# Group norm's last pieces and the weight turns one engine per step, and part of the last rounding to fp8 on GpSimd

## The chip, the cores and the metric

The kernel runs on one core of a Trainium2 chip. Its five engines each take their instructions from a queue of their own, in the order in which the program issued them: PE (TensorE, the matrix multiplier, whose results go to PSUM), DVE (VectorE), ACT (ScalarE), POOL (GpSimd) and SP (SyncE, used here to start DMAs). An engine that waits for another's result holds up everything behind it in its own queue. The metric is the device time of one execution in microseconds.

## The reference

The input is an image batch x of 4 x 64 x 64 positions with 96 channels; each image is a sequence of 4096 positions. Cut to what matters:

```python
# layer 0
xn   = layer_norm(group_norm(x, 32 groups of 3 channels))      # statistics of a whole image
proj = xn @ W_in + b_in                                        # 96 -> 3*96 + 3*96*16
h_t  = d_t * (A_t * h_{t-1}) + d_t * (B_t * u_t)               # a scan over 4096 positions, 96 x 16 states
y_t  = sigmoid(gate_t) * sum_over_16(C_t * h_t)
x    = x + y @ W_out + b_out
# layer 1
t = x + attention(layer_norm(x))                               # no softmax: q (k^T v), 6 heads
h = relu(q16(q8(ln(t)) @ q8(W1)^T) + q8(b1))                   # rounded to fp8 (5,2) before, fp16 after each product
t = t + q16(q16(q8(h) @ q8(W2)^T) + q8(b2))                    # 96 -> 384 -> 96
```

The group norm of an image needs sums over the whole image before its first position can be worked on, and the attention, being linear, needs a 97 x 97 matrix summed over the whole image before its first position can be finished.

## The kernel before

**Tiles and steps.** An image is cut into NCH = 8 chunks of 512 positions, so there are N = 32 chunks. A chunk's scan is cut into NT = 12 tiles of 128 partitions (32 channels times 4 states) by 512 positions. The main loop makes one *step* per tile, K = 384 in all. A step issues the tile's three projections (`project`, L269: three fp32r matmuls each, into the PSUM banks tagged A, B and C or D), ACT's copy of the B projection out of its single bank (`b_copy`, L811), POOL's product (`b_mul`, L814), DVE's product with d and bias (`a_mul`, L823), DVE's scan (L830), and the product with C on DVE (`c_mul`, L854) or on ACT and POOL (L860, L863).

**What hangs on the steps.** Everything else is put into a table `steps` by `at(step, fn)` and is issued at the end of that step. Offsets from a chunk's first step stand in the dictionary `AT`. `Front` prepares a chunk (group norm applied as `centre` and `scale` on POOL, L670 and L673; layer norm: `stats` L371 and L373 on DVE, `rstd` on POOL, L378 to L384, of which L392 is a power, `apply` on ACT, L396; `transpose`, L684; `affine`, `upper`, `low`; further projections). `tail` finishes a chunk of layer 0 (`state_sum` L878, `gated`, `project_out`, `residual` L926, a layer norm, `keep` L935 and `spill` of the transposed chunk to DRAM, `gram`). `attn_matrix` makes the image's 97 x 97 matrix `rmat`, and `ffn` does layer 1 of a chunk an image later: `fetch`, `attention` (L1076), `residual` (L1081), layer norm, `quant_in` (L1098), three products `hidden`, relu, rounding to fp8, `project_out` (L1133), `round_out`, `bias_out` (L1148), `total` (L1155), `store`. All PSUM tiles besides the projections share three banks tagged M; a new tile takes a bank that has been given back, and its first matmul waits for the last reader of the tile before.

**Group norm.** While image b is worked on, `group_norm(b+1, ...)` collects the sums of the next image: `first` (a chunk's mean as a shift, L564 and L566 on ACT), eight times `sums` (PE turns a chunk into a bank M) and `sums_out` (ACT, L574), and then a chain of small pieces. `moments` reduces on DVE (L581, L582) and goes on with three operations on POOL (L583 to L585); `mean` has a matmul (L590), two DVE operations (L592, L594) and, for images 1 to 3, two on POOL (L596, L597); `root` has a matmul (L602), one DVE operation (L604) and a power on POOL (L605); `diagonal` is on ACT (L612), `spread` on PE (L618), `spread_out` on ACT (L627). With e the step of the last `sums`, these stand at steps e+1, e+2, e+4, e+6, e+8 and e+8. All operations of a piece are issued in the same step, on three engines one after the other. For image 1, e is 57; for images 2 and 3 it is 149 and 245.

**Weight turns.** At steps 20, 32, 44 and 56 a matrix of layer 1 is turned by PE into a bank M and copied out by DVE in the same step; the last one, `weights_bias`, has four DVE operations (L355 to L359).

**The end.** Work whose step would be 384 or more is not put into the table. The last chunk's tail, what is left of image 2's layer 1 (chunks 5 to 7 above all) and all of image 3's layer 1 are given as jobs to a planner (`Plan`), each with an engine, an assumed cost and what it waits for. The planner lays out the jobs for a number of randomly disturbed priorities (`end.tries`), keeps the order that its own costs call the shortest, and issues the work in that order. For these chunks the relu is one DVE operation on fp16 (`relu_vector`, L1123), and `quant` (L1127) is one ACT operation that rounds a whole chunk, 128 x 1536, to fp8. In image 3 the layer norm of the even chunks is applied by DVE (L403) and of the odd ones by ACT (L396); `round_out` of the odd chunks is on DVE (L1141), of the even ones on ACT (L1143).

Of the kernel before, what the change touches and what calls it, by code (L numbers as in the profile page):

```python
# [63 lines left out]
def conv_attn_hybrid_kernel(  # L64
# [269 lines left out]
    def weights_attention():  # L334
        ps = bank("M", [C, CA], "wq_ps")
        nc.tensor.transpose(ps, w_qkv[:, 0:C], ident[:CA, :CA])
        nc.vector.tensor_copy(w_qt[0:C, :], ps)

    def weights_ffn1():
        ps = bank("M", [C, HID], "w1_ps")  # L340
        for m in range(NK):
            nc.tensor.transpose(ps[:, m * P : (m + 1) * P], w1_sb[:, m, :], ident)
        nc.vector.tensor_copy(w1_q, ps, saturate=False)

    def weights_ffn2():
        ps = bank("M", [P, NK, C], "w2_ps")
        for m in range(NK):
            nc.tensor.transpose(ps[:, m, :], w2_sb[:, m * P : (m + 1) * P], ident[:C, :C])
        nc.vector.tensor_copy(w2_q, ps, saturate=False)

    def weights_bias():
        ps = bank("M", [P, NK], "b1_ps")
        nc.tensor.transpose(ps, b1_sb, ident[:NK, :NK])
        b1_8 = small.tile([P, NK], F8, tag="b1_8", name="b1_8", bufs=1)
        nc.vector.tensor_copy(b1_8, ps, saturate=False)  # L355
        nc.vector.tensor_copy(b1_q, b1_8)
        b2_8 = small.tile([P, C], F8, tag="b2_8", name="b2_8", bufs=1)
        nc.vector.tensor_copy(b2_8, b2_sb, saturate=False)
        nc.vector.tensor_copy(b2_q, b2_8)  # L359
# [173 lines left out]
    class GroupNorm:  # L533
# [45 lines left out]
        def moments(self):  # L579
            t = small.tile([C, 2], F32, tag="gt", name=f"gt_{self.b}", bufs=2)  # L580
            nc.vector.tensor_reduce(t, self.s, AX.X, ALU.add)  # L581
            nc.vector.tensor_scalar_mul(t, t, 1.0 / L)  # L582
            nc.gpsimd.tensor_tensor(self.mv[:, 0:1], t[:, 0:1], self.c, ALU.subtract)  # L583
            nc.gpsimd.tensor_tensor(t[:, 0:1], t[:, 0:1], t[:, 0:1], ALU.mult)
            nc.gpsimd.tensor_tensor(self.mv[:, 1:2], t[:, 1:2], t[:, 0:1], ALU.subtract)  # L585


        def mean(self):
            ps = bank("M", [C, 2], f"gm_ps_{self.b}")
            nc.tensor.matmul(ps[:, 0:1], lhsT=third, rhs=self.mv[:, 0:1], start=True, stop=True)  # L590
            self.m = small.tile([C, 2], F32, tag="gm", name=f"gm_{self.b}", bufs=2)
            nc.vector.tensor_copy(self.m[:, 0:1], ps[:, 0:1])  # L592
            w = small.tile([C, 1], F32, tag="gw", name=f"gw_{self.b}", bufs=2)
            nc.vector.tensor_tensor(w, self.mv[:, 0:1], ps[:, 0:1], ALU.subtract)  # L594
            engine = nc.gpsimd if self.b else nc.vector
            engine.tensor_tensor(w, w, w, ALU.mult)  # L596
            engine.tensor_tensor(w, w, self.mv[:, 1:2], ALU.add)  # L597
            self.w = w

        def root(self):  # L600
            ps = bank("M", [C, 2], f"gv_ps_{self.b}")
            nc.tensor.matmul(ps[:, 0:1], lhsT=third, rhs=self.w, start=True, stop=True)  # L602
            v = small.tile([C, 1], F32, tag="gv", name=f"gv_{self.b}", bufs=2)
            nc.vector.tensor_scalar(v, ps[:, 0:1], 1e-5, None, ALU.add)  # L604
            nc.gpsimd.tensor_tensor(self.m[:, 1:2], v, mhalf[0:C, 0:1], ALU.pow)  # L605

# [22 lines left out]
    def group_norm(b, s0):  # L629
# [17 lines left out]
        for n in range(NCH):  # L647
# [3 lines left out]
            at(when[n] + AT["sums_out"] - AT["sums"], call, "sums_out", n)  # L651
        for n, name in ((1, "moments"), (2, "mean"), (4, "root"), (6, "diagonal"), (8, "spread"),
                        (8, "spread_out")):
            at(when[-1] + n, call, name)

# [237 lines left out]
    end.last = {}  # L893
    end.tries = 800

# [163 lines left out]
    def ffn(b, i, s0):  # L1059
# [6 lines left out]

        vector = b == B - 1 and i % 2 == 0

# [56 lines left out]
        def quant():  # L1125
            v["hq"] = sb("bu", [P, NK, TC], F8, f"hq_{nm}")
            nc.scalar.activation(v["hq"], v["h16"], AF.Copy, saturate=False)  # L1127

# [9 lines left out]
        def round_out():  # L1138
            v["y16"] = tile_of("y16", "xs", [P, J, C], F16, "y16")
            if phase["end"] and i % 2:  # L1140
                nc.vector.tensor_copy(v["y16"], v["ps"])  # L1141
            else:
                nc.scalar.copy(v["y16"], v["ps"])  # L1143

# [27 lines left out]
        if fetch not in done and b < B - 1:  # L1172
            at(K - 4, fetch)
            done.add(fetch)
# [24 lines left out]
        if hidden not in done:  # L1199
            r, h, c = [], None, None  # L1200
            for m in range(NK):
# [3 lines left out]
                        take=[f"rep:{nm}"] if m == 0 else [], free=[f"M:{m}{nm}"])  # L1205
                r.append(job("DVE", 0.5, relu_vector, m, after=[c]))
            a = job("ACT", 1.5, quant, after=r, take=[f"bu:q{nm}"], free=[f"rep:{nm}"])
        a = job("PE", 0.5, project_out, after=[a], take=[f"A:y{nm}"], free=[f"bu:q{nm}"])
        a = job(*(("ACT", 0.48) if vector else ("DVE", 0.56)), round_out, after=[a],
                take=[f"xs:{nm}"], free=[f"A:y{nm}"])  # L1210
# [11 lines left out]
    def planned_start():  # L1222
# [22 lines left out]
        a = job("DVE", 0.4, q.aggregate, after=a)  # L1245
        m = job("DVE", 1.1, q.mean, after=[a])
        r = job("DVE", 0.7, q.root, after=[m], late=0.9)
        g = []
# [119 lines left out]
    second = planned_start()  # L1368

    for n, fn in enumerate((weights_attention, weights_ffn1, weights_ffn2, weights_bias)):  # L1370
        at(NT + 8 + NT * n, fn)
    for b in range(B):
# [98 lines left out]
```

## Time and profile before

| | us |
|---|---|
| median of 3 runs | 1183.2 (1182.86 to 1183.66) |
| the profiled execution's own time | 1184.49 |
| its span in the trace | 1182.8 |
| PE busy | 1140.1 (96%) |
| DVE busy | 1113.2 (94%) |
| POOL busy | 1030.3 (87%) |
| ACT busy | 817.3 (69%) |

The span is the time from the first to the last instruction of the program; all stretches below are given in microseconds from its start. The steps run to about 1110; what follows is the planned end. "Busy" is time in which an engine executes; an instruction that waits is not busy. A row of the list of waits names the engine and line that waited, who released it, the total, the number of times and the longest. A row of a timeline has the start, the duration, the engine, the line, the operation, the tiles (out<-in), their shape, and in brackets how long the engine stood idle before it and what ended that. A row of the instruction groups ends in the busy time, the mean duration of one in ns, and the idle time before. A row of the table by stretch has the length, the busy time and count of instructions for PE, PEld (weight loads), DVE, ACT and POOL, then PE's granted clock, the DMA share and GB/s.

### The profile page before, as it was taken

How to read it: one execution, taken by the hardware profiler on the slowest of the kernel's cores; microseconds unless marked ns; L12 is line 12 of the kernel's file. 1: busy time of each engine (PE TensorE's matmuls, PEld its weight loads, DVE VectorE, ACT ScalarE, POOL GpSimd, SP SyncE). 2: the span in 40 equal slices, each digit the busy share in tenths (PEclk: the TensorE clock that was granted, in tenths of full speed). 3: DMA queues.
4: the chain of work that ended last, by engine and by line, in shares of the span. 5: the costliest groups of instructions: out<-in, count | busy, mean ns of one | idle time of the engine just before them, and what ended most of it. 6: DMA issues, size and time to landing. Idle time of an engine off the chain costs nothing. (4 is left out here: it accounts for less than half of the span.)

```text
span 1182.8 us, 19203 instructions
## 1 busy us (share of the span) xinstructions
PE 1140.1 (96%) x5899; PEld 874.6 (74%) x5899; DVE 1113.2 (94%) x2093; ACT 817.3 (69%) x1826; POOL 1030.3 (87%) x1176
## 2 busy tenths in 40 slices
PE   5999999999999999999999999999999999999885
PEld 4777777677777777777777777777777777777573
DVE  6999999899999999999999999999999999999865
ACT  4666655556556777877877777777776777776476
POOL 5798887788889899999999999999999999988554
PEclk8999999899999999999999999999999999999989
DMA  7676776687776776787777777766777778667221
GB/s 185 142 167 143 167 155 154 141 176 161 170 160 151 161 162 157 158 190 170 161 159 161 172 162 166 171 158 152 159 165 169 160 162 185 147 145 153 60 75 47
DMA packets 104288, 182.12 MB, mean 154 GB/s; under 512 B 42637, under 2 KB 50769, under 8 KB 104186
## 3 DMA queue, kind: packets, MB, share of 16 engines
q1 hardware_dynamic: 90060, 106.96, 37.3%
q0 software_dynamic: 13536, 73.93, 31.4%
q8 instruction: 46, 0.75, 0.3%
q14 instruction: 56, 0.46, 0.1%
q10 hardware_dynamic: 590, 0.02, 0.0%
HBM read 69.12 MB, written 24.77 MB: 79 GB/s over the span
## 5 line engine op out<-in xcount | busy, mean ns | idle before, releaser
L814 POOL TENSOR_TENSOR bu<-bu,rep 128x512 f32<-128x512 f32 x384 | 512.9, 1345 | 43.3 <-ACT state L840 34.8
L830 DVE TENSOR_TENSOR_SCAN h<-Aps,state,bu 128x512 f32<-128x512 f32 x336 | 426.2, 1268 | 0.7 <-POOL ch L863 0.5
L811 ACT ACTIVATE bu<-Bps,b_bac 128x512 f32<-128x512 f32 x384 | 263.1, 685 | 198.5 <-PE Bps L269 192.9
L823 DVE SCALAR_TENSOR_TENSOR Aps<-Aps,b_bac,rep 128x512 f32<-128x512 f32 x384 | 281.9, 734 | 8.2 <-PE Aps L269 8.2
L269 PE MATMUL Bps<-xs,w 128*128 128x512 f32 x768 | 268.0, 430 | 7.7 <-ACT bu L811 7.1
L269 PE MATMUL Aps<-xs,w 128*128 128x512 f32 x768 | 242.2, 396 | 1.2 <-DVE h L830 1.0
L863 POOL TENSOR_TENSOR ch<-ch,h 128x512 f32<-128x512 f32 x126 | 170.4, 1352 | 7.9 <-ACT ch L860 3.7
L269 PEld LDWEIGHTS Aps<-xs,w 128*128 128x128 f32 x768 | 143.9, 188 | 37.3 <-DVE h L830 3.0
L269 PEld LDWEIGHTS Bps<-xs,w 128*128 128x128 f32 x768 | 126.7, 191 | 51.2 <-ACT bu L811 15.4
L269 PE MATMUL Aps<-xl,w 128*128 128x512 f32 x384 | 152.0, 396 | 0.0
L269 PE MATMUL Bps<-xl,w 128*128 128x512 f32 x384 | 151.7, 395 | 0.0
L269 PE MATMUL Dps<-xs,w 128*128 128x512 f32 x384 | 121.0, 396 | 0.0
L269 PE MATMUL Cps<-xs,w 128*128 128x512 f32 x384 | 120.6, 395 | 0.0
L854 DVE SCALAR_TENSOR_TENSOR ch<-Dps,b_bac,h 128x512 f32<-128x512 f32 x160 | 118.6, 742 | 0.9 <-PE Dps L269 0.5
L869 POOL DMA_DIRECT2D ch<-ch x94 | 89.6, 953 | 0.3 <-DMA ch<-ch 0.3
L269 PEld LDWEIGHTS Bps<-xl,w 128*128 128x128 f32 x384 | 72.5, 189 | 17.7
L269 PEld LDWEIGHTS Dps<-xs,w 128*128 128x128 f32 x384 | 72.3, 188 | 17.7
L269 PEld LDWEIGHTS Aps<-xl,w 128*128 128x128 f32 x384 | 72.2, 188 | 17.7
L269 PEld LDWEIGHTS Cps<-xs,w 128*128 128x128 f32 x384 | 72.0, 188 | 17.6
L860 ACT ACTIVATE ch<-Cps,b_bac 128x512 f32<-128x512 f32 x94 | 64.6, 688 | 24.1 <-PE Cps L269 24.1
L269 PE MATMUL Dps<-xl,w 128*128 128x512 f32 x192 | 75.9, 395 | 0.0
L269 PE MATMUL Cps<-xl,w 128*128 128x512 f32 x192 | 75.8, 395 | 0.0
(200 smaller groups left out, 2045.2 us busy)
## 6 DMA issues: line engine op xcount, KB each, us to landing
ch<-ch POOLq DMA_DIRECT2D x94, 768.0 KB, 6.7
rep<-ddd SPq DMA_DIRECT2D x124, 384.0 KB, 7.4
ddd<-dd SPq DMA_DIRECT2D x31, 384.0 KB, 3.2
xl<-lo SPq DMA_DIRECT2D x62, 128.0 KB, 2.5
x<-in_x_dram SPq DMA_DIRECT2D x32, 192.0 KB, 3.0
xatd<-xat SPq DMA_DIRECT2D x32, 192.0 KB, 3.6
xal<-xatd SPq DMA_DIRECT2D x32, 192.0 KB, 2.8
out_dram<-o SPq DMA_DIRECT2D x32, 192.0 KB, 2.1
```

The lines of the kernel that those rows point to most:

```text
L269: nc.tensor.matmul(ps, lhsT=wt[:, n], rhs=mv, start=(n == 0), stop=(n == 2))
L811: nc.scalar.activation(self.bu, self.b_ps, AF.Identity, bias=self.bias(0))
L814: nc.gpsimd.tensor_tensor(self.bu, self.bu, rep[self.b, self.i][:, 1, self.cg], ALU.mult)
L823: nc.vector.scalar_tensor_tensor(self.a_ps, self.a_ps, self.bias(1), rep[self.b, self.i][:, 0, self.cg], ALU.add, ALU.mult,)
L830: nc.vector.tensor_tensor_scan(self.h, self.a_ps, self.bu, 0.0 if self.i == 0 else state[self.sh, self.cg], ALU.mult, ALU.add,)
L854: nc.vector.scalar_tensor_tensor(self.slot(), self.c_ps, self.bias(2), self.h, ALU.add, ALU.mult)
L860: nc.scalar.activation(self.ch, self.c_ps, AF.Identity, bias=self.bias(2))
L863: nc.gpsimd.tensor_tensor(self.ch, self.ch, self.h, ALU.mult)
L869: nc.gpsimd.dma_start(chs[g, 0], chs.pop((g, sh)), accum_op=ALU.add)
```

## The change

Three things are changed.

1. The group norm's chain is cut where the engine changes, into eleven pieces: moments (DVE), variances (POOL), group_sums (PE), mean (DVE), squares (POOL), group_sums (PE), offset (DVE), root (POOL), diagonal (ACT), spread (PE), spread_out (ACT). They stand one a step, at e+2, e+3, ... e+12. The PSUM tiles of group_sums and spread are now held from one step into the next. In the start of the kernel, which has a plan of its own, the pieces are called together in the old order.
2. Each weight turn's copy out of PSUM is issued one step after PE's transposes.
3. In the end, `quant` of the chunks with i % 3 != 0 is a POOL copy; DVE applies the layer norm only for i % 4 == 0 in image 3; all `round_out` are on ACT; the planner's cost of the relu is 0.47 for 0.5 and its tries are 1500 for 800. The fetch of image 2's last chunk is issued at step 383 for 380.

```diff
     def weights_attention():
         ps = bank("M", [C, CA], "wq_ps")
         nc.tensor.transpose(ps, w_qkv[:, 0:C], ident[:CA, :CA])
-        nc.vector.tensor_copy(w_qt[0:C, :], ps)
+        return lambda: nc.vector.tensor_copy(w_qt[0:C, :], ps)
...
             nc.vector.tensor_scalar_mul(t, t, 1.0 / L)
+            self.t = t
+
+        def variances(self):
+            t = self.t
             nc.gpsimd.tensor_tensor(self.mv[:, 0:1], t[:, 0:1], self.c, ALU.subtract)
...
+        def group_sums(self, name):
+            self.ps = bank("M", [C, 2], f"g{name}_ps_{self.b}")
+            nc.tensor.matmul(
+                self.ps[:, 0:1], lhsT=third, rhs=self.mv[:, 0:1] if name == "m" else self.w,
+                start=True, stop=True,
+            )
+
         def mean(self):
-            ps = bank("M", [C, 2], f"gm_ps_{self.b}")
-            nc.tensor.matmul(ps[:, 0:1], lhsT=third, rhs=self.mv[:, 0:1], start=True, stop=True)
+            ps = self.ps
...
+        def squares(self):
+            w, engine = self.w, nc.gpsimd if self.b else nc.vector
             engine.tensor_tensor(w, w, w, ALU.mult)
             engine.tensor_tensor(w, w, self.mv[:, 1:2], ALU.add)
-            self.w = w
+
+        def offset(self):
+            self.v = small.tile([C, 1], F32, tag="gv", name=f"gv_{self.b}", bufs=2)
+            nc.vector.tensor_scalar(self.v, self.ps[:, 0:1], 1e-5, None, ALU.add)

         def root(self):
-            ps = bank("M", [C, 2], f"gv_ps_{self.b}")
-            nc.tensor.matmul(ps[:, 0:1], lhsT=third, rhs=self.w, start=True, stop=True)
-            v = small.tile([C, 1], F32, tag="gv", name=f"gv_{self.b}", bufs=2)
-            nc.vector.tensor_scalar(v, ps[:, 0:1], 1e-5, None, ALU.add)
-            nc.gpsimd.tensor_tensor(self.m[:, 1:2], v, mhalf[0:C, 0:1], ALU.pow)
+            nc.gpsimd.tensor_tensor(self.m[:, 1:2], self.v, mhalf[0:C, 0:1], ALU.pow)
...
-        for n, name in ((1, "moments"), (2, "mean"), (4, "root"), (6, "diagonal"), (8, "spread"),
-                        (8, "spread_out")):
-            at(when[-1] + n, call, name)
+        chain = (
+            ("moments",), ("variances",), ("group_sums", "m"), ("mean",), ("squares",),
+            ("group_sums", "v"), ("offset",), ("root",), ("diagonal",), ("spread",), ("spread_out",),
+        )
+        for n, args in enumerate(chain):
+            at(when[-1] + AT["sums_out"] - AT["sums"] + 1 + n, call, *args)
...
-    end.tries = 800
+    end.tries = 1500
...
-        vector = b == B - 1 and i % 2 == 0
+        vector = b == B - 1 and i % 4 == 0
...
             v["hq"] = sb("bu", [P, NK, TC], F8, f"hq_{nm}")
-            nc.scalar.activation(v["hq"], v["h16"], AF.Copy, saturate=False)
+            if i % 3 == 0:
+                nc.scalar.activation(v["hq"], v["h16"], AF.Copy, saturate=False)
+            else:
+                nc.gpsimd.tensor_copy(v["hq"], v["h16"], saturate=False)
...
-            if phase["end"] and i % 2:
-                nc.vector.tensor_copy(v["y16"], v["ps"])
-            else:
-                nc.scalar.copy(v["y16"], v["ps"])
+            nc.scalar.copy(v["y16"], v["ps"])
...
-            at(K - 4, fetch)
+            at(K - 1, fetch)
...
-                r.append(job("DVE", 0.5, relu_vector, m, after=[c]))
-            a = job("ACT", 1.5, quant, after=r, take=[f"bu:q{nm}"], free=[f"rep:{nm}"])
+                r.append(job("DVE", 0.47, relu_vector, m, after=[c]))
+            a = job(*(("ACT", 1.5) if i % 3 == 0 else ("POOL", 1.6)), quant, after=r, take=[f"bu:q{nm}"], free=[f"rep:{nm}"])
...
+    def turned(step, fn):
+        at(step + 1, fn())
+
     for n, fn in enumerate((weights_attention, weights_ffn1, weights_ffn2, weights_bias)):
-        at(NT + 8 + NT * n, fn)
+        at(NT + 8 + NT * n, turned, NT + 8 + NT * n, fn)
```

`weights_ffn1`, `weights_ffn2` and `weights_bias` are changed as `weights_attention` is; the four DVE operations of `weights_bias` become a function `biases_out` that its lambda calls.

## The prediction

> **What bounds the kernel now.** I read the page first: PE is busy 96% of the span, DVE 94%. Between 230 and 1100 PE never rests, so there only a stall of PE, or work for PE, can move the time. The rest I looked for where the change works: the group norm chains (193 to 230 for image 1, 455 to 475 and 729 to 750 for images 2 and 3) and the end (1110 to 1177).
>
> The waits between 193 and 230 name what PE lost beside image 1's chain:
>
> ```profile
> PEld Bps L269 <- ACT bu L811: 3.0, 1, 3.0
> PE Bps L269 <- ACT bu L811: 2.6, 1, 2.6
> POOL gmv L583 <- DVE gt L582: 2.0, 1, 2.0
> ACT z L396 <- POOL nmr_c L384: 1.5, 1, 1.5
> PE xnt_ps L684 <- POOL bu L814: 0.9, 1, 0.9
> ```
>
> The timeline of that stall, in order of time:
>
> ```profile
> 207.45 0.58 POOL L605 TENSOR_TENSOR gm<-gv,mhalf 96x1 f32<-96x1 f32 x1
> ...
> 212.07 1.54 ACT L396 ACTIVATE z<-z,nmr_c,rstd_c 128x96 f32<-128x96 f32 x4 [1.53 <-POOL nmr_c L384]
> ...
> 213.51 0.63 ACT L612 ACTIVATE gdg<-ident,gm 96x96 f32<-96x96 f32 x2
> ...
> 214.88 0.67 ACT L811 ACTIVATE bu<-Bps,b_bac 128x512 f32<-128x512 f32 x1
> ...
> 215.61 1.22 PE L269 MATMUL Bps<-xs,w 128*128 128x512 f32 x2 [2.56 <-ACT bu L811]
> ```
>
> ACT's b_copy (L811), which frees the only bank B, stands behind a layer norm that waits for POOL, the chain's diagonal (L612) and the next image's `first`. The table by stretch shows what followed:
>
> ```profile
> 172.00:178.80 6.80, 5.71 (x26) 4.14 (x24) 6.80 (x16) 5.00 (x13) 5.78 (x9) 1.00 0.83 184
> 208.17:214.99 6.82, 4.87 (x24) 3.44 (x22) 6.29 (x14) 3.99 (x13) 6.65 (x10) 1.00 0.66 133
> 214.99:221.82 6.83, 6.21 (x17) 5.10 (x18) 3.86 (x4) 1.73 (x5) 3.58 (x3) 0.50 0.84 213
> ...
> 1142.00:1173.70 31.70, 23.17 (x190) 15.73 (x186) 21.39 (x75) 30.30 (x52) 17.09 (x24) 1.00 0.18 50
> ```
>
> After 6.8 us with 1.95 of them idle PE ran at clock 0.50 for 6.83 us; a stretch with 1.09 idle was followed by clock 1.00. The last row is the end: from 1142 ACT works 30.3 of 31.7 us, POOL 17.1. The groups of 1114 to 1178:
>
> ```profile
> L1127 ACT ACTIVATE hq<-h 128x1536 fp8e5<-128x1536 f16 x11 | 16.1, 1494 | 0.1
> L396 ACT ACTIVATE xn<-x,nmr_f,rstd_f 128x96 fp8e5<-128x96 f32 x24 | 9.3, 464 | 3.4 <-POOL nmr_f L384 3.4
> L1143 ACT CAST y<-y_ps 128x384 f16<-128x384 f32 x5 | 2.4, 487 | 0.9 <-PE y_ps L1133 0.9
> L1155 POOL TENSOR_TENSOR o<-x,yb 128x384 f32<-128x384 f32 x9 | 8.5, 954 | 0.5
> L1148 POOL TENSOR_TENSOR yb<-y,b_q 128x384 f16<-128x384 f16 x9 | 8.3, 922 | 7.6 <-ACT y L1143 5.9 <-DVE y L1141 1.6
> ```
>
> and, from the groups of POOL over the whole span, two that price a rounding there:
>
> ```profile
> L220 POOL MEMSET xn<- 128x512 fp8e5 x2 | 1.1, 528 | 0.1
> L208 POOL CAST ident<-ident 128x128 fp8e5<-128x128 f32 x1 | 0.3, 291 | 0.1
> ```
>
> **Part 1, image 1's chain.** The chain's pieces keep their durations and are only moved. The power (0.58) leaves POOL's queue ahead of rstd_c, and the diagonal leaves ACT's queue ahead of b_copy (`first` starts 0.54 after it). So b_copy ends 0.54 + 0.58 = 1.12 earlier, and PE's stall goes from 2.56 to 1.44. POOL also loses, a few steps earlier, three operations of 0.19 and two of 0.47 and 0.19; up to 1.2 more if POOL carries that forward. Idle in the stretch before 215 falls from 1.95 to 0.83, less than the 1.09 that left the clock at 1.00, so I take the halved clock as gone. Price of both: the two steps with the stall and the slow clock lasted 5.38 and 5.27 from one B projection to the next; the same two of the next chunk, without a chain, 2.43 and 2.55. The excess is 5.67, less 0.25 for the spread's matmul, which stays: 5.4. Left is the stall of 1.44: gain 4.0. It would be 1.1 if the clock is halved all the same, 5.2 if the 1.2 arrives too. The pieces meet no such crowd at their new steps (diagonal at 67, spread at 68): ACT is busy 15.2 of 30 us there. The chain ends at step 69; its first reader, centre, stands at 71.
>
> The Trainium skill (TensorE: Matmul & The Clock Gate, Part 1) lets the clock fall after an idle window of about 3.4 us. No gap here is that long (2.56 at most), yet the clock fell; by the page's rule the gain here would be the stall's 1.1 alone. I go by the row.
>
> **Part 1, images 2 and 3.** Before, POOL waits 0.59 for L604 (L605's row), and through the layer norm behind it PE stalls 0.65 in each: gone, -1.3. New: the mean's bank is held into the next step, so xnt (L684) gets the bank that ACT's keep (L935) has just read. Keep ran 463.75 to 464.33, xnt started at 464.23: 0.1 to 0.4 each, I take 0.2. New too: the diagonal (0.64) moves to the step of d_out, the layer norm and, for image 2, `first`, in ACT's queue ahead of b_copy. That ended at 483.12, PE's next B projection began at 483.17: +0.6; for image 3, 756.44 against 756.85: +0.2. Sum -1.3 + 0.4 + 0.8 = -0.1, bounds -1.3 and +2.
>
> **Part 2, the weight turns.** No engine's row shows a wait for PE by the copies, so nothing is gained; DVE's work is the same. One cover goes: the bank of weights_bias is now freed by L355 behind that step's scan, a_mul and c_mul. With the rows' durations (1.25, 0.73, 0.74) after 191.1, L355 ends near 193.9, and PE's xat turns (before at 193.24) wait for it: +0.7. In the other three turns the freed bank is not asked for before the copy. Bounds 0 and 1.2.
>
> **Part 3, the rounding's price.** A POOL memset of 512 columns takes 528, one of 128 takes 207: 0.84 ns a column. The cast of 128 columns takes 84 ns more than the memset, about what a one-column POOL operation costs (190, against 100 for a memset). So 291 + 1408 x 0.84 = 1.47 us. High by the cast's own slope from 100 ns: 2.39; far, by the two-input L1155 or L863: 3.7; low, if fp16 passes twice as fast: 0.8. I take 1.5, since the cast is the nearest row.
>
> The skill (GPSIMD Engine Reference, section 3.1) states 1.03 cycles an element at 1.2 GHz for a one-input body, an estimate of 1.32 us, and 2.6 for two inputs. Its section 8 speaks against the change: GpSimd and VectorE share their SBUF interfaces.
>
> This case shows such a cost: DVE's four pieces of xn (L403) took 1.03 us with POOL idle (1142.04) and 2.93 with POOL busy (1161.93); the relu has a median of 353 ns and a maximum of 899.
>
> **Part 3, the end.** Seven of eleven roundings leave ACT: -7 x 1.494 = -10.5. Eight more pieces of xn: +3.7. Six more casts of y: 6 x 0.487 = +2.9. ACT: -3.9. DVE loses 8 x 0.435 + 6 x 0.547 = 6.8; the relus' mean (0.41) may rise, bounds 0 and 33 x 0.49 = 16, I take +2, hidden by the 6.8. POOL gains 7 x 1.5 and four small operations (1.0): 11.5 on 35. In the changed order POOL still has, after the rounding of image 2's chunk 7: 7 yb, 8 o, 6 rstd (1.3 each), 4 nmr (0.5), 5 roundings, with 0.07 between instructions: 6.5 + 7.6 + 7.9 + 2 + 7.5 + 2.8 = 34.3. That chunk's relus ended at 1133.5; with a rounding off ACT and a cast on it I put them at 1132.5, the rounding at 1134.0, POOL's earliest end at 1168.3, against 1176.4 now: -8.1 if POOL never waits. So the gain lies between ACT's 3.9 and POOL's 8.1; I take 4.5, near ACT, since that engine was full. If POOL takes 2.39, its end moves by 5 x 0.9 = 4.5 and the gain is about 1. The fetch at step 383 is hidden: it lands in 2.8 us, its reader came at 1111.6, some 15 us later.
>
> **Sum.** -4.0 - 0.1 + 0.7 - 4.5 = -7.9. The profiled span is 1182.8 in an execution of 1184.49, 1.3 over the median, so I subtract from the median: 1183.2 - 7.9 = 1175.3.
>
> **Rivals.** A: POOL's rounding takes about 2.4, POOL bounds the end, which gains 1: 1183.2 - 4.0 - 0.1 + 0.7 - 1 = 1178.8. For it: POOL gets 46 of 60 us even at 1.5. Against: the cast's row. B: the clock is halved beside image 1's chain as before: gain 1.1 for 4.0: 1178.2. For it: 0.83 is not far under 1.09. C, slower: POOL rounds at the two-input price, 3.7 us. Its end is then 5 x 2.2 = 11 later than 1168.3, 1179.3, and with waits as now (3.5 us) 1182.8 instead of 1176.4: +6.4 - 3.4 = +3.0, 1186.2. It decides from where the end loses what the chain gains, a rounding of about 3.0. Against: no one-input row of POOL is so slow. D: the end's new order wins nothing and image 1's stall only shifts: 1182 to 1184.
>
> **How the numbers follow.** Forecast 0.66, A 0.10, B 0.07, D 0.08, C 0.09. Two runs can't be told apart below some 0.2% (2.4 us). Low: the chain's 5.2, -1.3, the end's 8.1, no new wait: 1168.6; I set 1169. High: takes in A, B and half of D: 1183. Faster 0.83 (forecast, A, B), same 0.08, slower 0.09.
>
> **What would show it.** In the waits near 215 PE's for b_copy under 1.5, clock 1.00 after it; a new PE wait of xat for L355 near 194 and small ones of xnt; no wait of L605; L1127's POOL group at about 1500; ACT some 45 us in the end; o last near 1172. The prediction is wrong if the rounding is over 2.4, if the halved clock shows up elsewhere in the steps, or if POOL's waits in the end grow beyond 4 us.

## The result, and the profile after

The changed kernel takes 1181.8 us (median of four runs, 1180.9 to 1184.47), the kernel before, on the same chip, 1183.0. The ratio is 0.9994 with a 95% interval of 0.9977 to 1.0012: no difference that can be measured. The profiled execution of the changed kernel took 1180.9, 0.9 under its median, with a span of 1179.2; that of the kernel before took 1184.49, 1.5 over its median. So the two traces lie 3.6 us apart, the medians only 1.2.

The two traces show two changes that work against each other. Up to the last tile's B projection the changed kernel is 5.4 us ahead (that projection starts at 1094.5 instead of 1099.9). From the end of the last scan (L852, before L830) to the end of the last sum `o` it needs 1.8 us more. Here is that stretch in the table by stretch, of the kernel before (columns as in the section on the profile: PE, PEld, DVE, ACT, POOL with their counts, clock, DMA, GB/s):

```profile
1109.65:1176.81 67.16, 54.47 (x399) 38.80 (x393) 44.64 (x171) 48.72 (x86) 34.57 (x52) 0.92 0.21 60
```

and of the kernel after:

```profile
1104.26:1173.23 68.97, 53.87 (x382) 38.10 (x376) 45.80 (x157) 45.52 (x93) 45.52 (x63) 0.87 0.21 58
```

ACT has 3.2 us less to do, as intended, but it now stands idle for 68.97 - 45.52 = 23.45 us, where it was idle for 18.44 before. The work left ACT, and the time did not follow it. POOL's idle time fell by 9.1 us.

The groups of the end after (line, engine, operation, tiles, count, then busy us, mean ns and the idle time before them) answer the prediction's list:

```profile
L1145 DVE TENSOR_SCALAR h<-h,b_q 128x512 f16<-128x512 f16 x33 | 15.8, 518 | 8.8 <-ACT h L1141 8.5
L399 ACT ACTIVATE xn<-x,nmr_f,rstd_f 128x96 fp8e5<-128x96 f32 x32 | 12.2, 460 | 1.8 <-POOL nmr_f L387 1.8
L1152 POOL CAST hq<-h 128x1536 fp8e5<-128x1536 f16 x7 | 10.3, 1468 | 4.5 <-DVE h L1145 4.5
L1150 ACT ACTIVATE hq<-h 128x1536 fp8e5<-128x1536 f16 x4 | 5.9, 1478 | 0.6 <-DVE h L1145 0.6
L406 DVE TENSOR_SCALAR xn<-x,mv_f,rstd_f 128x96 fp8e5<-128x96 f32 x8 | 5.7, 772 | 1.0 <-POOL rstd_f L395 1.0
L1165 ACT CAST y<-y_ps 128x384 f16<-128x384 f32 x11 | 5.2, 484 | 3.0 <-PE y_ps L1158 3.0
```

POOL's rounding costs 1468 ns, and the three ACT groups that change add up to 23.3 us against 27.8 before. What is new is DVE: a relu takes 518 ns instead of 411, a piece of `xn` 772 instead of 435. The two rows before are

```profile
L1123 DVE TENSOR_SCALAR h<-h,b_q 128x512 f16<-128x512 f16 x33 | 12.9, 411 | 4.7 <-ACT h L1119 3.6
L403 DVE TENSOR_SCALAR xn<-x,mv_f,rstd_f 128x96 fp8e5<-128x96 f32 x16 | 6.0, 435 | 0.0
```

Beside image 1's chain the waits after, 193 to 230 (who waited, who released it, total, times, longest), have these rows that the argument needs:

```profile
POOL rstd_c L381 <- DVE gw L607: 1.6, 1, 1.6
PE xnt_ps L706 <- POOL bu L836: 0.9, 1, 0.9
PE gv_ps L597 <- POOL gw L613: 0.8, 1, 0.8
PE xat_ps L953 <- DVE b L358: 0.3, 1, 0.3
```

The stall for b_copy (2.6 us for the matmul, 3.0 for its weight load) is gone. The table by stretch after shows what became of the clock, in the steps and in the end:

```profile
208.17:214.99 6.82, 6.06 (x30) 4.49 (x29) 6.82 (x17) 4.44 (x12) 5.75 (x10) 1.00 0.78 179
214.99:221.82 6.83, 6.83 (x34) 4.65 (x33) 6.38 (x9) 3.48 (x10) 5.56 (x6) 1.00 0.84 198
...
1114.47:1121.30 6.83, 4.85 (x42) 3.90 (x43) 5.12 (x21) 3.94 (x10) 3.96 (x7) 1.00 0.10 29
1121.30:1131.54 10.24, 10.24 (x51) 9.14 (x51) 4.70 (x22) 4.94 (x10) 5.23 (x11) 0.50 0.36 98
1145.19:1152.02 6.83, 4.70 (x34) 2.36 (x34) 6.08 (x10) 6.27 (x15) 5.59 (x5) 1.00 0.11 31
1152.02:1158.85 6.83, 6.20 (x38) 4.28 (x34) 5.43 (x15) 5.62 (x13) 6.50 (x7) 0.50 0.10 29
```

Before 215 PE idles 0.76 us instead of 1.95, and the clock stays at 1.00 there. In the end it is at 0.50 for 10.2 us, as before,

```profile
1126.35:1136.59 10.24, 10.24 (x51) 8.53 (x49) 5.90 (x30) 6.80 (x11) 5.84 (x10) 0.50 0.31 92
```

and for another 6.8 us from 1152, which the kernel before does not have.

Two places of the end show what this does. First, PE's and ACT's timelines after (start, duration, engine, line, operation; in brackets the idle time before it and what ended that):

```profile
1125.26 1.05 PE L1124 MATMUL h_ps<-xq,w_q 96*128 96x512 fp8e5 x2
1126.11 3.57 PE L1098 MATMUL a_ps<-rmat,xal 97*128 97x96 f32 x16
1129.47 0.63 PE L1124 MATMUL h_ps<-xq,w_q 96*128 96x512 fp8e5 x1
...
1130.14 0.59 ACT L1141 CAST h<-h_ps 128x512 f16<-128x512 f32 x1 [3.14 <-PE h_ps L1124]
```

The plan put sixteen matmuls of attention between a chunk's second hidden product and its third. At half clock they take 3.57 us, and ACT waits 3.14 us for the third product. Second, DVE and POOL after, in a stretch that leads to the last chunk:

```profile
1155.97 0.92 POOL L1170 TENSOR_TENSOR yb<-y,b_q 128x384 f16<-128x384 f16 x1
1156.84 1.46 POOL L1152 CAST hq<-h 128x1536 fp8e5<-128x1536 f16 x1
1158.26 0.91 POOL L1177 TENSOR_TENSOR o<-x,yb 128x384 f32<-128x384 f32 x1
1159.13 0.91 POOL L1170 TENSOR_TENSOR yb<-y,b_q 128x384 f16<-128x384 f16 x1
...
1156.03 4.08 DVE L406 TENSOR_SCALAR xn<-x,mv_f,rstd_f 128x96 fp8e5<-128x96 f32 x4 [0.98 <-POOL rstd_f L395]
1160.43 0.59 ACT L1120 ACTIVATE xq<-xq_ps 96x512 fp8e5<-96x512 f32 x1 [1.63 <-PE xq_ps L1113]
```

Four pieces of `xn` took 1.03 us where POOL was idle (the prediction has that number). Here they take 4.08, which is one piece for each of POOL's four instructions, and ACT waits for what follows from them.

### The profile page after: what moved, and what is told of

It is laid out like the page before. It is cut to its first block, busy times and chain, and to the rows that moved or that the text cites. A ratio compares the mean times of both kernels' runs of the same rounds, so it can differ in the third digit from the quotient of the medians.

```text
span 1179.2 us, 19184 instructions
## 1 busy us (share of the span) xinstructions
PE 1138.6 (97%) x5882; PEld 874.2 (74%) x5882; DVE 1113.3 (94%) x2079; ACT 812.9 (69%) x1833; POOL 1040.1 (88%) x1187
## 5 line engine op out<-in xcount | busy, mean ns | idle before, releaser
L852 DVE TENSOR_TENSOR_SCAN h<-Aps,state,bu 128x512 f32<-128x512 f32 x336 | 425.9, 1268 | 0.3 <-issue 0.2
```

What stands on the lines that cost most here:

```text
L852: nc.vector.tensor_tensor_scan(self.h, self.a_ps, self.bu, 0.0 if self.i == 0 else state[self.sh, self.cg], ALU.mult, ALU.add,)
```

## The experiments

Three theories came out of these traces. L: an instruction of DVE is held behind POOL's long ones, and more work on POOL means more of that. K: PE's clock is halved for longer, because the plan leaves PE fewer filling products. (The planner puts junk matmuls, `awake`, into the gaps that its plan shows for PE, each gap less 0.4 us, one for every 0.4 us. The plan before was 69.1 us long and had 56 of them, the plan after is 63.7 long and has 39.) C: the order that the random tries come to is good or bad by chance. (The expectations of the first four runs call L and C 1a and 1b; the next four put two others, A and B, beside C and say what they are.) All runs, each against the kernel before on its chip:

| kernel | median us | before us | ratio, 95% interval |
|---|---|---|---|
| changed kernel | 1181.8 | 1183.0 | 0.9994, 0.9977 to 1.0012 |
| steps | 1179.6 | 1183.6 | 0.9968, 0.9956 to 0.9980 |
| endonly | 1187.6 | 1183.6 | 1.0031, 1.0021 to 1.0041 |
| quant | 1175.4 | 1183.6 | 0.9933, 0.9921 to 0.9945 |
| moves | 1180.2 | 1183.6 | 0.9967, 0.9955 to 0.9980 |
| quant_moves | 1176.6 | 1184.2 | 0.9934, 0.9923 to 0.9946 |
| quant_tries | 1184.0 | 1184.2 | 1.0005, 0.9996 to 1.0015 |
| after_s3 | 1180.6 | 1184.2 | 0.9969, 0.9958 to 0.9980 |
| quant_s2 | 1179.6 | 1184.2 | 0.9961, 0.9947 to 0.9975 |
| after_thirds | 1181.9 | 1183.3 | 0.9987, 0.9977 to 0.9996 |
| after_awake2 | 1179.6 | 1183.3 | 0.9964, 0.9950 to 0.9978 |
| after_awake | 1179.4 | 1183.3 | 0.9963, 0.9950 to 0.9977 |
| after_both | 1179.0 | 1183.3 | 0.9960, 0.9947 to 0.9974 |
| qm_awake | 1172.4 | 1183.7 | 0.9901, 0.9888 to 0.9914 |
| qt_awake | 1179.6 | 1183.7 | 0.9968, 0.9956 to 0.9979 |
| after_800 | 1180.1 | 1183.7 | 0.9968, 0.9959 to 0.9977 |
| steps_awake | 1178.0 | 1183.7 | 0.9953, 0.9939 to 0.9966 |
| after_x0 | 1177.9 | 1183.4 | 0.9952, 0.9938 to 0.9965 |
| qm_both | 1173.3 | 1183.4 | 0.9914, 0.9901 to 0.9928 |

0.001 of the ratio is 1.2 us.

### Steps and end apart

`steps` has parts 1 and 2 of the change and the end of before; `endonly` has part 3 alone.

> The group norm's pieces and the turns of the weights as in the changed kernel, the end as before. Theory 1 (the steps gained 5.4 us and the new end lost 1.8 or more of it): 1183.0 - 5.4 = about 1177.6, the last B projection starting near 1065 us as in the changed kernel, and 68.3 us from there-abouts to the last sum as in the kernel before (from the xat gap that DVE's copy ends). Rival (the end costs the same whatever its order, and it only starts earlier or later; what the changed kernel lost comes from how the steps leave the queues when the end begins): about 1181.8, as the changed kernel.

> The end as in the changed kernel (rounding of chunks on POOL, the moves, 1500 tries), the steps as before. Theory 1: the end is longer by 1.8 us or more whatever stands before it, so 1183.0 + 1.8 to + 4 = 1184.8 to 1187. Rival (the end is no longer by itself, 68.3 us): 1183.0 within 0.7. My forecast's own term (-4.5) would give 1178.5.

`steps` gained 0.32% (3.8 us; its profiled execution has its last B projection at 1094.9, 5.0 ahead of that of before); its 1179.6 lies between the two expectations. `endonly` lost 0.31%, a little more than expected. So the two parts add up, within the intervals, to what the whole change shows, and where the forecast had -4.5 for the end, the runs show +3.7.

### The end, part by part

`quant` takes the steps and, of part 3, only this:

```diff
-            nc.scalar.activation(v["hq"], v["h16"], AF.Copy, saturate=False)
+            if i % 3 == 0:
+                nc.scalar.activation(v["hq"], v["h16"], AF.Copy, saturate=False)
+            else:
+                nc.gpsimd.tensor_copy(v["hq"], v["h16"], saturate=False)
```

with the job of `quant` on POOL in the plan. `moves` takes the steps and only this, its jobs moved in the plan too:

```diff
-        vector = b == B - 1 and i % 2 == 0
+        vector = b == B - 1 and i % 4 == 0
...
-            if phase["end"] and i % 2:
-                nc.vector.tensor_copy(v["y16"], v["ps"])
-            else:
-                nc.scalar.copy(v["y16"], v["ps"])
+            nc.scalar.copy(v["y16"], v["ps"])
```

> The steps of the changed kernel, and of the changes to the end the rounding of two chunks of three on POOL alone (its order is planned anew). Theory 1a (POOL full, and its instructions slow DVE's: relu 411 to 518 ns, xn 1.0 to 4.1 us): this part is what lost the time, so the end is 2 to 5 us longer than with the steps alone, 1179.5 to 1182.5. Theory 1b (the loss is chance in the order that the plan comes to, such as both products of attention put ahead of the third hidden one): the end comes out anywhere within 3 us of the steps alone, with DVE's relu at 500 ns or more all the same. My forecast's queue sums (ACT 16.1 us of rounding down to 5.9) would give 4 us less than the steps alone, 1173.5.

> The steps of the changed kernel, and of the changes to the end only that chunks 2 and 6 are normalised by ACT in place of DVE and that ACT rounds every y: all roundings to fp8 stay on ACT. Theory 1a (only POOL's roundings cost): ACT has some 2.9 + 2.8 us more of work (xn 9.3 to 12.2, y 2.4 to 5.2), DVE less; ACT has idle time in the end, so 0 to 5 us longer than the steps alone, 1177.6 to 1182.6, with DVE's relu at 411 ns as before. Theory 1b (chance of the order): within 3 us of the steps alone to either side.

The rounding on POOL alone brings 0.35% over the steps, 4.1 us: nearly what I had forecast for the whole of part 3. The moves alone bring nothing and cost nothing. Theory L in its plain form (each rounding on POOL costs) has fallen: the same seven roundings stand in `quant`. Then both together, and the rounding with what is left of part 3 (the planner's 1500 tries, its relu cost of 0.47 and the later fetch). `quant_moves` against the changed kernel:

```diff
-    end.tries = 1500
+    end.tries = 800
...
-                r.append(job("DVE", 0.47, relu_vector, m, after=[c]))
+                r.append(job("DVE", 0.5, relu_vector, m, after=[c]))
...
-            at(K - 1, fetch)
+            at(K - 4, fetch)
```

`quant_tries` against `quant`:

```diff
-    end.tries = 800
+    end.tries = 1500
...
-                r.append(job("DVE", 0.5, relu_vector, m, after=[c]))
+                r.append(job("DVE", 0.47, relu_vector, m, after=[c]))
...
-            at(K - 4, fetch)
+            at(K - 1, fetch)
```

and two kernels that change nothing but the planner's random numbers, the changed kernel with `random.Random(3)` and `quant` with `random.Random(2)`:

> The steps, the rounding on POOL and the moves of layer norm and y to ACT, without the third part (800 tries, relu at 0.50 in the plan, the early fetch). The plan's own length of the end is 65.6 (69.1 before, 65.8 with the rounding alone, 63.7 for the whole change). Theory A (the moves spoil the gain of the rounding: one POOL rounding beside DVE's relus and ACT's normalisations): as the whole change, 1181 to 1183. Theory B (the third part spoils it: 1500 tries and the shorter relu cost choose an order that is shorter in the plan and longer on the chip): as the rounding alone, 1175 to 1176. Theory C (chance of the order): anywhere from 1175 to 1183.

> The steps, the rounding on POOL and the third part (1500 tries, relu at 0.47, the fetch at K - 1), without the moves to ACT. The plan's own length is 64.4. Theory A: as the rounding alone, 1175 to 1176. Theory B: 1181 to 1183. Theory C: anywhere from 1175 to 1183.

> The whole change, with the planner's random numbers begun from 3 instead of 1; the work, the costs and the number of tries are the same, and the plan's own length is 64.4 in place of 63.7. Theories A and B (the work is what costs): 1181 to 1183, as the changed kernel. Theory C (which order the tries come to is what costs): more than 2 us away from it, most likely below, 1175 to 1180.

> The steps and the rounding on POOL alone, random numbers begun from 2; the plan's own length is 65.3 in place of 65.8. Theories A and B: 1175 to 1176, as with the first numbers. Theory C: more than 2 us away, most likely above, 1177 to 1183.

`quant_moves` has all the work of the changed kernel, engine by engine, and is 7 us faster. `quant_tries` is 8.5 us slower than `quant`. The relu's cost and the tries act on nothing but the planner's order. The later fetch acts on the chip, but not on this time: in the changed kernel's trace it is issued before 1081.1, no transfer of its line takes more than 7.9 us to land, and the matmuls that read it start at 1107.97. So what loses the time is not the work that part 3 moves but the order in which the planner issues it. Other random numbers alone move the time by 3 us (0.0025 and 0.0028). Theory A has fallen; B and C hold in part, since the third part leads to the slowest orders and chance moves any of them. One more kernel undid only the number of tries (800 for 1500 in the changed kernel):

> The whole change with 800 tries in place of 1500, and so another order, 65.3 long in the plan, 43 fillings. If the larger number of tries is what spoils the order (the shorter the plan, the fewer its fillings and the less slack): 1177 to 1180. If the order is chance: anywhere from 1176 to 1184.

It lies at 0.9968, 3 us better than the changed kernel, at the edge of the first expectation and inside the second. I put the seven orders that have POOL's roundings together, by the length that the plan gives itself:

| order | plan us | filling products | ratio |
|---|---|---|---|
| quant | 65.8 | 50 | 0.9933 |
| quant_moves | 65.6 | 45 | 0.9934 |
| after_800 | 65.4 | 43 | 0.9968 |
| quant_s2 | 65.3 | 45 | 0.9961 |
| after_s3 | 64.4 | 38 | 0.9969 |
| quant_tries | 64.4 | 39 | 1.0005 |
| changed kernel | 63.7 | 39 | 0.9994 |

The shorter the plan, the slower the kernel, very nearly in order. Part of that may come with the relu's cost: the changed kernel, `quant_tries`, `after_s3` and `after_800` were planned with 0.47, the other three with 0.5, and `quant_moves` and `after_800`, with the same work and tries and nearly the same length, lie 4 us apart. The changed kernel's 1500 tries found an order that is better by the planner's costs than that of its 800, and worse on the chip. Seven orders are few, but they suggest that the planner's costs leave something out that its search then runs into.

### What the plan leaves out: PE's clock

Here the order stays as it is in each kernel, and only more filling products are issued: 62 in `after_awake2`, 81 in `after_awake`, against 39.

```diff
-                    for _ in range(int(max(0.0, t - self.time.get(e, t) - 0.4) / 0.4)):
+                    for _ in range(int(max(0.0, t - self.time.get(e, t) + 0.2) / 0.4)):
```

(`after_awake2` has neither the - 0.4 nor the + 0.2.) The same edit as in `after_awake` was made in the order of `quant_moves` (`qm_awake`), of `quant_tries` (`qt_awake`) and in the end of before (`steps_awake`).

> The whole change in its own order, with more filling products on PE: one for every 0.4 us of a gap of the plan (62) where the changed kernel takes 0.4 us off each gap first (39). Theory K: less halved clock in the end (17 us in the changed kernel's trace, 10 in that of before), the 3.6 us of two chunks' attention back towards 2, ACT's wait of 3.1 us for the third hidden product shorter by about as much: 1178 to 1181. Theory L: no shorter, 1182 to 1184, and the fillings can hold back real products by some 0.2 us each.

> As the run with 62 fillings, but 81: one more in nearly every gap. Theory K: the clock stays at 1.00 for all of the end; 9 us or so of PE's time come back, but 42 fillings of 0.39 us are 16 us of new work in gaps that the chip does not always have; 1177 to 1182. Theory L: 1183 to 1186.

> Rounding on POOL and the moves in the order of 800 tries (1176.6 without more fillings, its clock halved for 24 us of the end in its trace), with 85 fillings in place of 45. Theory K (halved clock adds to any order): full clock through the end, 2 to 4 us shorter, 1172.5 to 1174.5. If the halved windows of this order lie where nothing waits for PE: 1176 to 1177. From the changed kernel's order with the same fillings (0.9963 of before, 1179.4) the difference that is left, 3 us or more, would be the order's own.

> The steps, the rounding on POOL and the third part without the moves (1184.0, the slowest with the steps; clock halved for 27 us, relus at 612 ns), with 80 fillings in place of 40. Theory K alone: the 7 to 8 us above the rounding alone go with the halved clock, 1176 to 1178. Theory L (what this order puts of DVE's relus beside POOL's long instructions costs, 8.8 us of relus above 346 ns each): clock full and still 1180 to 1182, relus above 550 ns.

> The steps of the change, the end as before, with 93 fillings in place of 57. Theory K: the end of before has halved windows too (10 us), so it gains 1 to 2 us as well, 1177.5 to 1178.5 against 1179.6. If only the new orders suffer from the clock: 1179.6 within 0.7.

Four orders, and each gains: the changed kernel's 0.31% (3.7 us; 0.30% with 62 fillings), that of `quant_moves` 0.33%, of `quant_tries` 0.37%, the old end 0.15% (there the two intervals overlap). In the changed kernel's order the executions also lie closer together, 1178.8 to 1179.6 with 81 fillings against 1180.9 to 1184.5 without; in that of `quant_tries` they still spread from 1178.7 to 1183.8. In the trace of `after_awake` the clock and the sixteen matmuls read

```profile
1121.30:1131.50 10.20, 9.88 (x80) 8.03 (x80) 7.68 (x39) 7.71 (x16) 7.72 (x13) 1.00 0.36 100
```

```profile
1124.81 1.03 PE L1098 MATMUL a_ps<-rmat,xal 97*128 97x96 f32 x8
1126.03 1.10 PE L1098 MATMUL a_ps<-rmat,xal 97*128 97x96 f32 x8 [0.19 <-ACT h L1141]
...
1127.39 0.58 ACT L1141 CAST h<-h_ps 128x512 f16<-128x512 f32 x1 [1.36 <-PE h_ps L1124]
```

At full clock they take 2.1 us instead of 3.57, and ACT's wait falls from 3.14 to 1.36. Theory K is shown: in the changed kernel's order, keeping the clock up brings 3.7 us. It explains less of what that order lost against the old end, which also gains 1.8 us with fillings: with fillings in both, the changed kernel is 1.2 us behind instead of 3.1 (0.9963 against 0.9953, within the intervals). Nor is it all that the orders differ in: with the clock repaired, the order of `quant_moves` is at 0.9901 and that of the changed kernel at 0.9963, 7.3 us apart with the same work. `qt_awake` stayed at 0.9968, between what the two theories had expected; its profiled execution, 1183.8 against a median of 1179.6, still has 14 us of halved clock, so it does not tell them apart.

### What the plan leaves out: DVE behind POOL

`after_thirds` keeps the changed kernel's order and issues each rounding of POOL as three instructions; `after_both` has that and 81 fillings, and `qm_both` the same two in the order of `quant_moves`.

```diff
-                nc.gpsimd.tensor_copy(v["hq"], v["h16"], saturate=False)
+                for m in range(NK):
+                    nc.gpsimd.tensor_copy(v["hq"][:, m, :], v["h16"][:, m, :], saturate=False)
```

> The whole change in its own order; only each rounding on POOL is issued as three instructions of 512 values in place of one of 1536, so that none keeps POOL for 1.47 us at a time. Theory L (a relu, a normalisation or a sum on DVE that begins while POOL runs one of its long instructions takes until that one is over: in the traces so far relus alone took 346 ns and beside hq up to 1622): relus and xn beside hq take at most about 0.9 us, their mean falls from 517 and 772 ns towards 430 and 500, and the end is 2 to 4 us shorter: 1179 to 1181. Theory K (PE's clock, halved for 17 us of the end, with 39 filling products in place of 56): about 1183, as the changed kernel by its ratio to the kernel before on this chip (1183.9).

> The whole change in its own order with roundings in thirds and 81 fillings. If both theories hold in part, the two gains add up: 1175 to 1178. If the order itself is bad (attention of two chunks ahead of a third hidden product, and the last chunks' yb and o ahead of the first's relus on DVE), 1182 or more remain.

> The fastest so far (rounding on POOL and the moves in the order of 800 tries, 85 fillings, 1172.4) with POOL's roundings in thirds. In the changed kernel's order thirds brought 0.4 to 0.8. Theory L: 1171.5 to 1172. If POOL's 2.8 us of additional work meets this order's own bound: 1172.5 to 1174.

In the timeline of `after_thirds` the same stretch as above:

```profile
1157.31 1.73 POOL L1153 CAST hq<-h 128x512 fp8e5<-128x512 f16 x3
...
1156.51 2.59 DVE L406 TENSOR_SCALAR xn<-x,mv_f,rstd_f 128x96 fp8e5<-128x96 f32 x4 [0.98 <-POOL rstd_f L395]
1159.02 2.95 DVE L1145 TENSOR_SCALAR h<-h,b_q 128x512 f16<-128x512 f16 x3
```

`xn` takes 1.5 us less, but the three relus behind it now meet POOL's next instructions and take 2.95 us where they took 1.52. In the whole end the pieces of `xn` fell from 772 to 670 ns, the relus rose from 518 to 545, and POOL has 2.1 us more to do (a third takes 623 ns). The time moves by 0.07%, within the intervals, and so do `after_both` against `after_awake` (0.03%; expected at 1175 to 1178, it took 1179.0) and `qm_both` against `qm_awake` (0.13%, the other way). My expectation of 2 to 4 us was wrong: in the stretch shown, shorter POOL instructions only change which of DVE's are held. What POOL's additional work costs was not run by itself. The last kernel takes one such stretch off DVE, in the order with 81 fillings: chunk 0 alone is normalised by ACT, at the same place of the order.

```diff
-            (ln.apply_vector if vector else ln.apply)(v["xn"], t, saturate=False)
+            (ln.apply_vector if vector and i else ln.apply)(v["xn"], t, saturate=False)
```

> The changed kernel's own order with 81 fillings, and chunk 0 alone normalised by ACT in place of DVE at the same place of the order (in the trace with 81 fillings DVE took 4.08 us for it at 1153.81, each of its four instructions ending within 0.1 us of one on POOL, and ACT stood idle 2.35 us for what comes of it). Theory L: that chain gets shorter by 2 us or so, 1176.5 to 1178 (1179.4 with 81 fillings alone). If it only moves the wait (ACT has 1.7 us more to do in front of the next chunk): 1179 to 1180.

Its ACT timeline:

```profile
1154.50 1.54 ACT L399 ACTIVATE xn<-x,nmr_f,rstd_f 128x96 fp8e5<-128x96 f32 x4 [0.28 <-POOL nmr_f L387]
1155.95 0.46 ACT L1165 CAST y<-y_ps 128x384 f16<-128x384 f32 x1
1156.31 1.54 ACT L399 ACTIVATE xn<-x,nmr_f,rstd_f 128x96 fp8e5<-128x96 f32 x4
1157.75 0.58 ACT L1120 ACTIVATE xq<-xq_ps 96x512 fp8e5<-96x512 f32 x1
```

The first row is chunk 0's normalisation, 1.54 us; the second `xn` is the last chunk's, which ACT had before as well. ACT goes on to chunk 0's `xq` without a pause, where it waited 2.35 us in `after_awake`. The median is 1.5 us lower than that of `after_awake` and 0.11% by the ratios, whose intervals overlap; size and trace agree with theory L, but it is not shown.

The rest, some 6 us between `after_x0` and `qm_awake`, is in the order too. Longer relus do not tell the two orders apart: they take 539 ns on the mean in `qm_awake` and 541 in `after_awake`. The eight pieces of `xn` do, 356 against 773 ns, 3.3 us in all. Half of the rest can be read in ACT's idle time, and none of it was tried. These are the two ends from the last scan to the last sum, of `after_awake`

```profile
1104.40:1171.87 67.47, 57.03 (x424) 39.49 (x418) 46.52 (x157) 45.38 (x93) 45.65 (x63) 0.97 0.21 60
1152.10:1171.87 19.77, 13.64 (x95) 8.77 (x91) 11.93 (x19) 12.27 (x22) 12.28 (x13) 0.90 0.19 51
```

and of `qm_awake`, with its last part from the same distance of 47.7 us behind the scan:

```profile
1104.95:1167.12 62.17, 53.74 (x416) 38.17 (x414) 42.31 (x157) 44.92 (x93) 44.66 (x63) 0.99 0.23 67
1152.65:1167.12 14.47, 9.92 (x84) 6.53 (x82) 8.16 (x13) 10.37 (x21) 10.97 (x12) 0.96 0.18 50
```

ACT and POOL have the same work to within 1 us. In the last part ACT is idle for 7.5 us in the one and 4.1 in the other: the changed kernel's order ends with chunks whose normalisation, relus and sums follow one another with nothing beside them.

## Why the prediction was wrong

Forecast 1175.3 and faster by 0.7%; measured 1181.8, no difference.

**Image 1's chain, -4.0: right, in part by luck.** The two steps with the stall lasted 5.38 and 5.27 us before and 3.31 and 2.55 after, so -4.8; the twelve tiles of that chunk took 39.81 and now 35.59, so -4.2. The stall of 1.44 for b_copy that the forecast left in place did not come; PE's wait for `gv_ps` (0.76) was not forecast and is part of the 3.31. The clock stayed at 1.00, so rival B is out. But the line that this was read from, 1.09 us of idle time in 6.8, is no safe one: the changed kernel lost the clock at 1121.30 after 3.41 us with 1.05 idle, and `quant_moves` kept it through 3.41 us with 1.68 idle (1150.92 to 1154.33) and after them. The clock page of the Trainium skill (TensorE: Matmul & The Clock Gate, Part 1) would have given 1.1; the row was the better guide.

**Images 2 and 3, -0.1: the gain was put too low.** Each of the two periods is 0.54 shorter (35.99 to 35.45, 35.03 to 34.49), -1.1 together. PE's stalls went, as forecast; the +0.8 for the diagonal in ACT's queue did not come, because PE was not waiting for that b_copy: the waits after, 455 to 490 and 729 to 765, have no row of PE's matmuls. **Weight turns, +0.7: too high.** PE's new wait for L358 is there, 0.25 us (it lies inside the -4.2). Together these steps were forecast at -3.4 and were -5.4 in the profiled executions and -3.8 in the whole time of the run with the steps alone.

**The rounding's price, 1.5: right.** 1468 ns by seven instructions. Rivals A and C are out. Where the skill's page (GPSIMD Engine Reference, section 3.1) stands behind an estimate of 1.32, the measurement decides.

**The end, -4.5: wrong, +3 to +4.** This is the step that failed. I added up what leaves ACT and what stays on POOL, and set the end's change between -3.9 and -8.1. ACT's sum was nearly right: -3.2 in the whole stretch. But a sum of busy times gives the change of the end only if the idle times stay what they were. I took "if POOL never waits" as one bound and ACT's sum as the other, so that no bound stood on the side of a loss, and ACT's sum alone had all of ACT's 18.44 us of waits unchanged. They rose to 23.45. The planner had made a wholly new order by fixed costs that don't follow two things seen in these traces: PE's clock, for which the shorter plan even issued 17 fewer filling products (keeping it up brings 3.7 us), and DVE's waits behind POOL (seen, their price not shown). What else makes one order 7 us faster than another with the same work stays open. I had both things in front of me. The prediction shows the clock falling after 6.8 us with 1.95 idle, but applies it to the steps alone; it shows `xn` at 2.93 instead of 1.03 beside a busy POOL, and then hides +2 us of relus under the 6.8 that DVE loses. In the stretch shown above there was no such cover: what was held was on the way to ACT's next instruction, which waited 1.63 us.

**Rival D** named the outcome (1182 to 1184, by a new order that wins nothing) with a chance of 0.08, but coupled it with a stall that only shifts. The stall went; the order alone did it. After the runs it would have the larger part of the chance, since other random numbers move this end by 3 us, and all seven orders lie within 8.5.

The forecast's own number was reached after all, by the rounding alone (1175.4) and by the same work in another order (1176.6). With the clock kept up that order takes 1172.4, 0.9901 of the kernel before: faster than both kernels.

## What to carry to other kernels

A sum of work moved off the fullest engine is a forecast for the end of a kernel only where the order stays; where a planner makes a new order, ask first what its costs leave out, and do not take a shorter plan for a shorter run. In this kernel a plan 1.9 us shorter was 7 us slower with the same work. When idle gaps of PE are filled by the plan's clock, count the gaps on the chip as well: a shorter plan with the same waits leaves PE idle where nothing fills it.

## What the runs showed of the hardware that I had not expected

**The clock falls without a long gap, and differs between executions of one program.** The two halved stretches of the changed kernel's end follow 6.83 us in which PE was idle for 2.0 and 2.1 us in all, in gaps of at most 0.93 and 0.69 us. The sum of idle time alone does not tell when it falls, as the two stretches of 3.41 us in the section above show. Each halved stretch that was over before the last sum, in the ten traces before the fillings, lasted a multiple of 3.4 us. The same order of the end had it at 12 to 16, 19 to 22, 36 to 40, 46 to 53 and 57 to 63 us behind the last scan in `endonly`, and at 17 to 27 and 48 to 55 in the changed kernel. The twelve executions of `quant_tries` had mean granted clocks from 0.976 to 0.985 and took 1183.3 to 1188.6 us. In the changed kernel's order 81 fillings took most of that spread away along with the loss.

**Some of DVE's operations on SBUF wait for whole instructions of POOL.** I took all relus of the first ten traces (the two kernels and the eight runs up to `quant_s2`). The 209 beside which POOL ran no `hq`, `yb` or `o` took 318 to 385 ns. Beside one of these they took up to 1622, and in the stretch shown above each piece of `xn` ended within 0.1 us of one of POOL's instructions. DVE's own last sums `o` took 557 ns alone and 1147 to 1297 behind POOL. It goes the other way too: the eight `o` of POOL that began while DVE's `yb` ran took 1.17 to 1.30 us, where their median in the kernel before is 0.92. DVE's residual, which reads PSUM (554 ns with POOL idle, 544 beside `hq`), and its statistics, which read SBUF (245 and 245), did not change. The Trainium skill says the same of DVE's operations in a mode that uses two ports or with two SBUF inputs (SBUF — State Buffer, the section on two separate sides): whichever of the two engines starts first holds the pair of ports that they share for its whole instruction, and the other is blocked, not slowed. In these traces that is so for the relus, the normalisations and the sums; which modes the instructions ran in, no run here shows.
